# Row-halved output blocks in context attention, self-attention's last softmax steps reordered, and the gated weights' column sums in eight halves

## The chip, the cores and the metric

The kernel runs on one core of a Trainium2 chip. The metric is the device time of one execution in microseconds. The core's engines appear in the profile as PE (TensorE, matmuls; its weight loads are shown apart as PEld), DVE (VectorE), ACT (ScalarE), POOL (GpSimd) and SP (SyncE, whose queue issues nearly all DMAs here). Everything is in float32.

## The reference

The inputs are x (2 batches x 1024 tokens x 256) and a context of 2 x 154 rows of width 192. One transformer block is computed: self-attention with 16 heads of 64, attention over the context with 16 heads of 64, and a gated feed-forward part of inner width 1024, each behind a layer norm and with a residual.

```python
def _attention(xq, xkv, wq, wk, wv, wo, bo):
    q = (xq @ wq).reshape(B, S, N_HEADS, D_HEAD)
    k = (xkv @ wk).reshape(B, T, N_HEADS, D_HEAD)
    v = (xkv @ wv).reshape(B, T, N_HEADS, D_HEAD)
    attn = softmax(einsum('bihd,bjhd->bhij', q, k) * D_HEAD ** (-0.5), axis=-1)
    out = einsum('bhij,bjhd->bihd', attn, v).reshape(B, S, D_ATTN)
    return out @ wo + bo
h = _layernorm(x, ln1_g, ln1_b)
x = _attention(h, h, sa_wq, sa_wk, sa_wv, sa_wo, sa_bo) + x
h = _layernorm(x, ln2_g, ln2_b)
x = _attention(h, cond_emb, ca_wq, ca_wk, ca_wv, ca_wo, ca_bo) + x
h = _layernorm(x, ln3_g, ln3_b)
a, gate = split(h @ ff_w1 + ff_b1)
h = a * gelu(gate) @ ff_w2 + ff_b2
return h + x
```

## The kernel before

The order of every instruction on every engine is the order of the program text: the schedule is written out by hand, and nothing is moved by a planner. The stages are the first norm and projections, self-attention, context attention, and the feed-forward part. Stages overlap: steps of one are put between steps of its neighbours by lists of closures. `adds`, `stores`, `lates`, `side` and `later` are such lists. `stores` holds copies of finished PSUM banks to SBUF, `adds` the additions of finished output blocks to the residual, `later` DMAs that go out at most two a step, and `side` transposes of the next norm's output and other work of TensorE. `run_work(...)` runs what is due from these lists.

PSUM is divided into three pools. The pool of products has two banks (`mm_tile`): query projections, transposes. The pool of sums has two banks (`sum_tile`): output blocks, sums over steps. The pool of scores has two double banks. A tile of a pool waits until the tile two before it in that pool was read to the end.

**Self-attention** runs in 128 steps (SA = 128). The softmax of a step is spread over engines: `maxima` and `turn_group` (the transposes of the weighted exponentials, L733) on VectorE, `exponents` (L600) on ScalarE, `differences` and `softmax_join` (the denominators, L629) and `weighted` (L706) on GpSimd, `reciprocals` (L698) and `factors` on VectorE. The weighting of a step's second half may also run on ScalarE (`weighted_beside`). Its output projection (`out_rounds`, L547) is done in rounds of four blocks of 128 tokens. TensorE works there as an array of eight tiles of 64 rows x 32 columns: the two row halves (the two heads of a pair) write to two different banks at the same time. After a first crossing of each pair of banks, ScalarE reads one element of the first bank of the pair (`seen`, L556), and the second crossing then lets each row half add to the other's bank. So a round takes four banks, two of the sums and two of the products.

**Context attention** runs in units. A unit is a pair of heads of one batch: 16 units, batch 0 in units 0 to 7, batch 1 in units 8 to 15. A unit has three steps n = 0, 1, 2 that take 3, 3 and 2 blocks of 128 queries (CG). A step c = 3 ui + n issues its scores (`cross_first`, L999, K = 64 rows), the maxima over VectorE (L1004), the exponentials on ScalarE (L1017), and the weighting on GpSimd (L1028). The transposes follow two steps later (`cross_drain`), and the products with the values (`cross_values`, L1064, array of 32 x 64 tiles, four banks) come at step 0 two units later. Beside that, in the program's order:

- n = 0: the values of the unit two before, then a piece of `side`.
- n = 1: the query projection of the next unit (`cross_queries`, L411: 64 rows x 128 columns, two row halves at once on the two banks of the products), which ScalarE copies out (`take_both`, L426) at the next step.
- n = 2: an output piece, a value projection (even units), a piece of `side` or an output piece, the flush of the copies, and another output piece.

The output projection is cut into pieces of two blocks of 128 tokens (`out_piece`, L523: K = 128 rows, one bank of the sums, 8 matmuls for both blocks and both pairs of heads). Those of self-attention's last pairs of heads run in units 1 and 2, those of context attention's in later units, where an odd unit above 2 lists the pieces of the two units before (`cross_beside`), and those of the last two pairs in the feed-forward part. The bias and norm of the next stage can only start on a block once all its additions are made (`norm_beside`, the statistics on VectorE).

The context's values are projected with the 192 context columns as two halves of CC = 96 rows, `context_values(b, pr)` (L961), once per batch and even pair, eight times in all: one at self-attention's end and one in each even unit. ScalarE copies the result out (L968), and DMAs take it through memory in order to spread it over the four row groups that L1064 wants.

The **feed-forward** part computes 32 pairs of blocks with gates (L1169, 1187 to 1219) in 64 half steps k, and the second matrix by a Strassen-Winograd scheme (seven products for eight, final sums at L1289). For it VectorE forms four sums of quarters of ff_w2 (`column_sums`, L1256, 128 x 512 elements each) at k = 5 to 8. Statistics of the last norm of batch 1 run on VectorE in the half steps k = 10 and later.

## Time and profile before

| what | value |
|---|---|
| times of three runs | 1059.89, 1060.45, 1060.54 us (median 1060.45) |
| the profiled execution | 1060.44 us, its span 1058.6 us |
| busy share of the span | PE 99%, DVE 83%, POOL 73%, ACT 62% |
| context attention | first scores at 687.57 us of the span, last values at 900.44 us |

A line of the grouped view gives line, engine, operation, output <- inputs, tile (rows x columns in the array, where given), shape, count | busy us, mean ns of one | idle time before it and what ended it. A line of the timeline gives start and duration in us from the span's start, then engine, line, operation and the number of instructions that the row takes together; a bracket says how long the row's first instruction waited and for whom. Durations of matmuls of two row halves overlap, so their number times the mean is more than the time that they take together.

### The profile page before, as it was taken

The page shows a single profiled execution, that of the slowest core. Times are in us where ns is not written, and L with a number is a line of the kernel's source. Part 1 is how long each engine was busy: PE and PEld are TensorE (multiplying, and loading weights), DVE is VectorE, ACT ScalarE, POOL GpSimd, SP SyncE. Part 2 cuts the span into 40 slices and gives each one's busy share as a digit, 9 for nine tenths or more (in the row PEclk, how much of TensorE's full clock was granted, in tenths as well). Part 3 has the DMA queues.
Part 4 walks back from the last instruction along what each step waited for, and adds up shares of the span by engine and source line. Part 5 has one row for each costly group of instructions (what it writes and reads, how often), then busy time and mean ns, then how long its engine had stood idle before and what let it go on. Part 6 is the DMA issues. An engine that isn't in the chain of part 4 may idle for free.

```text
span 1058.6 us, 51303 instructions
## 1 busy us (share of the span) xinstructions
PE 1047.1 (99%) x21700; PEld 740.3 (70%) x21700; DVE 880.7 (83%) x1313; ACT 658.9 (62%) x2147; POOL 769.9 (73%) x1620
## 2 busy tenths in 40 slices
PE   8999999999999999999999999999999999999998
PEld 6456965556576666665786676666676667889997
DVE  5799999999899999999999999968776777675654
ACT  5776767777776766766776777666666655243221
POOL 2677777788778777777777777757665777598773
PEclk9999999999999999999999999999999999999999
DMA  4322221121121021122122012135323221000000
GB/s 106 95 65 60 50 61 42 45 54 34 25 54 45 15 54 45 29 44 55 24 44 50 21 39 56 49 104 132 101 59 83 69 59 41 1 11 11 21 11 30
DMA packets 96023, 52.87 MB, mean 50 GB/s; under 512 B 30314, under 2 KB 93810, under 8 KB 95794
## 3 DMA queue, kind: packets, MB, share of 16 engines
q1 hardware_dynamic: 94466, 48.93, 18.9%
q8 instruction: 171, 2.80, 1.1%
q10 hardware_dynamic: 1328, 0.66, 0.2%
q14 instruction: 58, 0.48, 0.1%
HBM read 36.23 MB, written 4.39 MB: 38 GB/s over the span
## 4 chain that ended last, share of the span: by engine, by line
PE 90%; DVE 4%; ACT 2%; POOL 2%; issue 1%; DMA 1%; SPq 0%; DVEq 0%; POOLq 0%; ACTq 0%
PE s L583 20%; PE po L639 20%; PE pv_sa L443 5%; PE py_ca L523 5%; PE pk_sa L411 5%; PE pq_sa L411 5%; PE pr L547 5%; PE pf L1289 5%; PE poc L1064 4%; PE pb L1169 4%; PE pq_ca L411 4%; PE sc L999 3%; PE pa L1169 2%; PE pc L1169 2%; PE ph_ln L323 1%
## 5 line engine op out<-in xcount | busy, mean ns | idle before, releaser
L600 ACT ACTIVATE p<-s,st 128x512 f32<-128x512 f32 x512 | 345.4, 685 | 152.8 <-DVE st L592 121.4
L706 POOL TENSOR_SCALAR p<-p,rd,ee 128x512 f32<-128x512 f32 x508 | 385.2, 768 | 75.5 <-DVE rd L698 75.1
L592 DVE TENSOR_REDUCE st<-s 128x2 f32<-128x1024 f32 x256 | 308.7, 1207 | 49.9 <-issue 16.1
L733 DVE STREAM_TRANSPOSE pT<-p 128x1024 f32<-128x1024 f32 x256 | 303.9, 1221 | 2.4 <-POOL p L706 2.3
L583 PE MATMUL s<-k_sa,q_sa 64*32 64x512 f32 x4096 | 256.7, 590 | 1.1 <-DVE k_sa L432 0.6
L639 PE MATMUL po<-pT,v_sa 64*32 64x256 f32 x6144 | 180.5, 376 | 1.7 <-ACT p L1017 1.6
L639 PEld LDWEIGHTS po<-pT,v_sa 64*32 64x32 f32 x6144 | 142.7, 106 | 45.0 <-issue 15.2
L583 PEld LDWEIGHTS s<-k_sa,q_sa 64*32 64x32 f32 x4096 | 102.8, 106 | 78.5 <-issue 51.4
L1017 ACT ACTIVATE p<-sc,neg 128x154 f32<-128x154 f32 x256 | 97.1, 406 | 72.2 <-DVE rden L1025 70.2
L1028 POOL TENSOR_SCALAR p<-p,rden 128x154 f32<-128x154 f32 x256 | 96.8, 399 | 52.9 <-DVE rden L1025 51.9
L600 ACT ACTIVATION_READ_ACCUMULATOR p<-s,st 128x1 f32 x512 | 103.0, 201 | 0.0
L1004 DVE TENSOR_REDUCE neg<-sc 128x6 f32<-128x924 f32 (+1 forms) x48 | 48.1, 1003 | 20.2 <-PE sc L999 20.0
L523 PE MATMUL py_ca<-ca_wo,o_ca 128*128 128x256 f32 x256 | 61.1, 385 | 0.0
L639 PE MATMUL po<-pT,third_v 64*32 64x256 f32 x2048 | 60.5, 376 | 0.0
L443 PE MATMUL pv_sa<-sa_wv,home 64*32 64x256 f32 x2048 | 60.2, 376 | 0.0
L443 PEld LDWEIGHTS pv_sa<-sa_wv,home 64*32 64x32 f32 x2048 | 48.4, 106 | 14.1 <-issue 5.4
L411 PE MATMUL pq_sa<-home,sa_wq 64*32 64x512 f32 (+1 forms) x976 | 58.0, 586 | 0.0
L411 PE MATMUL pq_ca<-home,ca_wq 64*128 64x512 f32 (+1 forms) x352 | 57.8, 589 | 0.0
L639 PEld LDWEIGHTS po<-pT,third_v 64*32 64x32 f32 x2048 | 46.6, 106 | 16.0 <-issue 4.6
L1017 ACT ACTIVATION_READ_ACCUMULATOR p<-sc,neg 128x1 f32 x256 | 56.5, 221 | 0.0
L627 POOL TENSOR_TENSOR zz<-ee,st 128x8 f32<-128x8 f32 x128 | 25.8, 202 | 42.1 <-ACT ee L625 42.1
L411 PE MATMUL pk_sa<-home,sa_wk 64*32 64x512 f32 x960 | 56.3, 589 | 0.0
(144 smaller groups left out, 1576.1 us busy)
## 6 DMA issues: line engine op xcount, KB each, us to landing
st<-st SPq DMA_DIRECT2D x510, 1.0 KB, 1.7
v_sa<-v_sa SPq DMA_DIRECT2D x24, 256.0 KB, 3.3
v_ca<-vd SPq DMA_DIRECT2D x32, 160.0 KB, 3.4
sa_wq<-in_L_xattn_sa_wq_dram SPq DMA_DIRECT2D x32, 128.0 KB, 3.3
sa_wk<-in_L_xattn_sa_wk_dram SPq DMA_DIRECT2D x32, 128.0 KB, 3.1
sa_wv<-in_L_xattn_sa_wv_dram SPq DMA_DIRECT2D x32, 128.0 KB, 3.3
ca_wq<-in_L_xattn_ca_wq_dram SPq DMA_DIRECT2D x32, 128.0 KB, 3.0
wf<-in_L_xattn_ff_w_dram SPq DMA_DIRECT2D x12, 256.0 KB, 4.8
```

The costliest lines, as they stand in the source:

```text
L411: nc.tensor.matmul(pq[r][f:f + m, at:at + n], lhsT=wt[own, c, f:f + m], rhs=h[own, c, t0:t0 + n], start=(c == 0), stop=(c == NH - 1), tile ...
L443: nc.tensor.matmul(pv[r][f:f + KB, i * VC:(i + 1) * VC], lhsT=h[own, c, t0:t0 + KB], rhs=wt[own, c, :], start=(c == 0), stop=(c == NH - 1) ...
L523: nc.tensor.matmul(py[:, e * D:(e + 1) * D], lhsT=o[:, i, (t + e) * P:(t + e + 1) * P], rhs=wo[kind, b, g][:, i, :], start=(i == 0), stop= ...
L583: nc.tensor.matmul(sc[a4 * KB:(a4 + 1) * KB, j, :], lhsT=q[r, c:c + KB], rhs=k[r, h * HB:(h + 1) * HB], start=True, stop=True, tile_positi ...
L592: nc.vector.tensor_reduce(st[:, 0, 0, i, :], sc, AX.X, ALU.max, negate=True)
L600: nc.scalar.activation(pr[:, j, :], sc[:, j, :], AF.Exp, bias=st[:, 0, 0, i, j:j + 1], accum_out=st[:, 0, 1, i, j:j + 1],)
L639: nc.tensor.matmul(po[a2][d:d + KB, :QH // 2], lhsT=v[r, t, e, d:d + KB], rhs=pT[r, d // DH * NK + n, :], start=(t == 0 and e == 0), stop= ...
L706: nc.gpsimd.tensor_scalar(pr[:, j, :], pr[:, j, :], v["rd"][:, c:c + 1], v["ee"][:, 0, c:c + 1], op0=ALU.mult, op1=ALU.mult,)
L733: nc.vector.transpose(halves[h][:, :, c:c + KB], slot[p]["members"][i].rearrange("p j (n k) -> p (j n) k", k=KB))
L1017: nc.scalar.activation(pr_[:, j, i, :T], sc[:, j, i * T:(i + 1) * T], AF.Exp, bias=neg[:, j, i:i + 1], accum_out=den[:, j, i:i + 1],)
L1028: nc.gpsimd.tensor_scalar(pr_[:, j, i, :T], pr_[:, j, i, :T], rden[:, j, i:i + 1], 1.0, op0=ALU.mult, op1=ALU.mult,)
L1169: nc.tensor.matmul(into[:, :BT], lhsT=lhs, rhs=wh[pair][i], start=first, stop=True, skip_group_check=True)
```

## The change

Five edits belong together.

1. `out_rounds` takes the kind of attention and a block width m. With m = P = 128 it does four blocks of tokens in 32 matmuls of 64 rows x 128 columns, two at a time, on the same four banks as in self-attention. `four_by_four` lists such rounds of four blocks. In units 1 and 2 (self-attention's last output; both rounds in unit 1, at n = 1 and n = 2), in units 7 to 11 (n = 2) and in unit 15 (n = 1) a round takes the place of the two pieces of two blocks. Where the next norm's transposes are due in that step (`beside`), in units 3 to 6 and 12 to 15, the step keeps pieces of 128 rows, and the side work runs at n = 2 only there. In the feed-forward part the pieces stay. The first crossings are issued behind the step's scores, the second crossings between the step's exponentials (`then(between)`: the first before the first head's exponentials and the second before the second head's), and the additions behind the step.
2. `context_values(pr, bank)` projects the values of both batches at once, with three pieces of 64 rows, the two row halves on two banks. That needs the context and its weights in another place: `context_beside` copies the context's columns to `both_ctx` by eight DMAs within SBUF, in units 3 to 6 of self-attention, and `load_weights` loads the value weights twice, for the two row halves. It is called four times, at self-attention's end and in units 2, 4 and 6. Batch 1's units only fetch their values from memory (`hold_values`, `spread_values`).
3. At self-attention's end the last two softmax steps (SA - 2 and SA - 1), which had been finished in context steps 0 and 1, are interleaved in another order: both reciprocals and weightings are issued in step 0, ahead of one or both transposes that had stood before them, and the last step's transposes move to the head of step 1, ahead of its maxima.
4. In unit 2's last step the output piece that had stood ahead of the value projection is gone with the first edit.
5. `column_sums` makes the four sums as eight halves of 128 x 256 elements, at k = 8 to 15.

```diff
@@ load_weights
-            wsl[kind, pr, what] = load_slice(f"{kind}_w{what}", pr * P, VC, CC)
+            t = wsl[kind, pr, what] = wpool.tile(
+                [P, DC // HR, VC], F32, tag="wv", name=f"{kind}_w{what}_{pr}")
+            own = w[f"{kind}_w{what}"][:, pr * P:pr * P + VC].rearrange("(c p) f -> p c f", p=HR)
+            for r0 in range(0, P, HR):
+                nc.sync.dma_start(out=t[r0:r0 + HR], in_=own)
@@
-    def out_rounds(b, g, tiles):
-        o = oT["sa", b, g]
+    def out_rounds(kind, b, g, tiles, m=KB):
+        o = oT[kind, b, g]
...
-                for f in range(0, P, KB):
+                for f in range(0, P, m):
                     for r in (1, 0):
                         at = 2 * pair + (r ^ swapped)
                         own, t0 = slice(r * HR, (r + 1) * HR), tiles[at] * P + f
                         nc.tensor.matmul(
-                            py[at][f:f + KB, :D], lhsT=o[own, i, t0:t0 + KB],
-                            rhs=wo["sa", b, g][own, i, :],
+                            py[at][f:f + m, :D], lhsT=o[own, i, t0:t0 + m],
+                            rhs=wo[kind, b, g][own, i, :],
...
+    rounds = []
+    def four_by_four(kind, b, g):
+        pairs = out_order(kind)
+        for i in range(0, len(pairs), 2):
+            rounds.append((kind, b, g, [t + e for t in pairs[i:i + 2] for e in range(2)]))
@@ turn_group
-        if i == 1:
+        slot[p]["left"] = slot[p].get("left", 2) - 1
+        if not slot[p]["left"]:
             del slot[p]
@@ self-attention's steps
+        if both and ui > SH - 2 and n in ((SH + 1, SH + 2) if ui % 2 else (0, 1)):
+            both.pop(0)()
@@
-    def context_values(b, pr, bank=mm_tile):
-        v = vs["ca", b, pr // 2] = pt_.tile([P, NB, VC], F32, tag="V", name=f"v_ca{b}_{pr}")
-        pv = bank(f"pv_ca{b}_{pr}")
-        for c in range(2):
-            nc.tensor.matmul(
-                pv[:, :VC], lhsT=ctxT[:, c, b * TP:b * TP + P],
-                rhs=wsl["ca", pr, "v"][:, c, :], start=(c == 0), stop=(c == 1),
-            )
+    both_ctx = ends[:, :DC // HR * P].rearrange("p (c k) -> p c k", k=P)
+    def context_beside():
...
+                    moves.append(lambda b=b, c=c, half=half, row=row, n=n, to=to: nc.sync.dma_start(
+                        out=both_ctx[to:to + n, c, :],
+                        in_=ctxT[row:row + n, half, b * TP:b * TP + P]))
...
+    def hold_values(b, pr):
+        v = vs["ca", b, pr // 2] = pt_.tile([P, NB + B, VC], F32, tag="V", name=f"v_ca{b}_{pr}")
+        return v
+    def spread_values(b, pr, at):
+        def back(a0):
+            for a4 in range(a0, a0 + 2):
+                nc.sync.dma_start(
+                    out=vs["ca", b, pr // 2][a4 * KB:(a4 + 1) * KB, :NB, :],
+                    in_=vd[b, pr].rearrange("(n p) d -> p n d", p=KB))
+        later.insert(at, lambda: back(0))
+        later.insert(at + 1, lambda: back(2))
+    def context_values(pr, bank):
+        v = hold_values(0, pr)
+        pv = [bank(f"pv_ca{b}_{pr}") for b in range(B)]
+        for c in range(DC // HR):
+            for b in range(B):
+                own = slice(b * HR, (b + 1) * HR)
+                nc.tensor.matmul(
+                    pv[b][:, :VC], lhsT=both_ctx[own, c, :], rhs=wsl["ca", pr, "v"][own, c, :],
+                    start=(c == 0), stop=(c == DC // HR - 1), tile_position=(b * HR, 0))
...
         def store():
+            for b in range(B):
+                nc.scalar.copy(v[:, NB + b, :], pv[b][:, :VC])
+            later.insert(0, lambda: [out(b) for b in range(B)])
+            spread_values(0, pr, 2)
@@ cross_first
-        def then(between=None):
+        def then(between=()):
...
-                if j and between:
-                    between()
+                for fn in between[j:j + 1] if len(between) > 1 else between if j else ():
+                    fn()
@@ cross_beside
-            out_pieces("ca", *divmod(ui // HP - 1, NQ), out_order("ca"))
+            four_by_four("ca", *divmod(ui // HP - 1, NQ))
@@ column_sums
-        t = half["t"]
+        n, part = divmod(n, 2)
+        t, own = half["t"], slice(part * NF // 4, (part + 1) * NF // 4)
...
+        nc.vector.tensor_tensor(into[:, own], x[:, own], y[:, own], ALU.subtract)
@@ the steps of context attention
-                out_pieces("sa", B - 1, NQ - 1, out_order("sa"))
+                four_by_four("sa", B - 1, NQ - 1)
...
-                load_weights("ca", nxt[1], "v")
+                if not nxt[0]:
+                    load_weights("ca", nxt[1], "v")
             flush(adds)
-            between = None
-            if c < 2:
-                if c == 0:
-                    turn_group(SA - 3, 1)
-                reciprocals(SA + c - 2)
-                factors(SA + c - 2)
+            between, taken = (), ()
+            if c == 0:
+                turn_group(SA - 3, 1)
+                reciprocals(SA - 2)
+                factors(SA - 2)
+            elif c == 1:
+                for i in range(2):
+                    turn_group(SA - 1, i)
             then = cross_first(c)
-            if c < 2:
-                weighted(SA + c - 2, 0)
-                weighted_beside(SA + c - 2, 1)
-                if c == 0:
-                    slot[SA - 1]["dd"] = differences(SA - 1, slot[SA - 1]["st"])
-                    between = lambda: softmax_join(SA - 1)
+            if c == 0:
+                weighted(SA - 2, 0, (0,))
+                weighted_beside(SA - 2, 1)
+                slot[SA - 1]["dd"] = differences(SA - 1, slot[SA - 1]["st"])
+                weighted(SA - 2, 0, (1,))
+                softmax_join(SA - 1)
             flush(stores)
             flush(lates)
             if n == 0 and ui > 1:
...
             else:
+                beside = n == 2 and side and side[0][0] and added.issuperset(side[0][1])
+                if rounds and (n == 2 or n == 1 and (ui == 1 or not nxt)):
+                    if beside:
+                        kind, ob, og, tiles = rounds.pop(0)
+                        out_pieces(kind, ob, og, tiles[::2])
+                    else:
+                        between, taken = out_rounds(*rounds.pop(0), P)
                 lates.append(then(between))
-            if c < 2:
-                turn_group(SA + c - 2, 0)
-                turn_group(SA + c - 2, 1)
+            if c == 0:
+                turn_group(SA - 2, 1)
+                reciprocals(SA - 1)
+                factors(SA - 1)
+                weighted(SA - 1, 0)
+                weighted_beside(SA - 1, 1)
+                turn_group(SA - 2, 0)
             cross_drain(c)
...
-                if ui == 1 or not nxt:
-                    run_work(2, 0)
-                else:
+                if ui > 1 and nxt:
                     run(lambda: cross_queries(*nxt))
                 run_work(0, 1)
             else:
                 run_work(0, 0, n_sum=1)
                 flush(adds)
-                if ui and ui % 2 == 0:
-                    run(lambda: context_values(*units[ui]))
-                run_work(0, 1, mm_tile)
+                if beside:
+                    run_work(0, 1, mm_tile)
                 flush(stores)
-                if ui > 1:
-                    run_work(0, 0, n_sum=1)
+                run_work(0, 0, n_sum=1)
+                if ui and ui % 2 == 0 and not b:
+                    run(lambda: context_values(ui, mm_tile))
+                elif b and ui % 2 == 0:
+                    hold_values(*units[ui])
+                    spread_values(*units[ui], 0)
...
+            adds.extend(taken)
@@ the feed-forward part's half steps
-            if len(CG) + 1 < k <= NF:
-                column_sums(k - len(CG) - 2)
+            if NF <= k < 2 * NF:
+                column_sums(k - NF)
```

More of the change, by code (lines that the diff above doesn't have):

```diff
@@ L807, in self_first @@
         return then
-    held, kept, rounds = [], [], []
+    held, kept = [], []
     def self_beside(ui):
@@ L828, in self_beside @@
             ob, og = divmod(ui // HP - 1, NQ)
-            for t0 in range(0, NG * 2, 2):
-                rounds.append(
-                    (ob, og, [t + e for t in out_order("sa")[t0:t0 + 2] for e in range(2)]))
+            four_by_four("sa", ob, og)
         if ui in (4, 6):
@@ L952, in context_ends @@
         return store
-    def context_values(b, pr, bank=mm_tile):
-        v = vs["ca", b, pr // 2] = pt_.tile([P, NB, VC], F32, tag="V", name=f"v_ca{b}_{pr}")
-        pv = bank(f"pv_ca{b}_{pr}")
-        for c in range(2):
-            nc.tensor.matmul(
-                pv[:, :VC], lhsT=ctxT[:, c, b * TP:b * TP + P],
-                rhs=wsl["ca", pr, "v"][:, c, :], start=(c == 0), stop=(c == 1),
-            )
-        def store():
-            own = one.tile([P, VC], F32, tag="own_v", name=f"own_v{b}_{pr}")
-            nc.scalar.copy(own, pv[:, :VC])
-            later.insert(0, lambda: nc.sync.dma_start(out=vd[b, pr][:P, :], in_=own))
-            def back(a0):
-                for a4 in range(a0, a0 + 2):
-                    nc.sync.dma_start(
-                        out=v[a4 * KB:(a4 + 1) * KB, :, :],
-                        in_=vd[b, pr].rearrange("(n p) d -> p n d", p=KB))
-            later.insert(2, lambda: back(0))
-            later.insert(3, lambda: back(2))
+    both_ctx = ends[:, :DC // HR * P].rearrange("p (c k) -> p c k", k=P)
@@ new lines, in context_beside @@
+    def context_beside():
+        moves = []
+        for b in range(B):
+            for c in range(DC // HR):
+                f = c * HR
+                while f < (c + 1) * HR:
+                    half, row = divmod(f, CC)
+                    n = min((c + 1) * HR - f, CC - row)
+                    to = b * HR + f - c * HR
+                    moves.append(lambda b=b, c=c, half=half, row=row, n=n, to=to: nc.sync.dma_start(
+                        out=both_ctx[to:to + n, c, :],
+                        in_=ctxT[row:row + n, half, b * TP:b * TP + P]))
+                    f += n
+        return moves
@@ L1419, in tile_transformer_block @@
                     hold_late_keys()
-                    run(lambda: context_values(*units[0]))
+                    run(lambda: context_values(0, mm_tile))
                     for pr in range(NKD, NPAIR):
```

18 lines of the change are left out of this document (13 added, 5 removed).

## The prediction

> **What bounds the kernel now.** I read the page's busy line first, then the groups of instructions by line and form, then the timeline of TensorE through context attention, with ScalarE and VectorE beside it where TensorE and they meet.
>
> ```profile
> PE 1047.1 (99%) x21700; PEld 740.3 (70%) x21700; DVE 880.7 (83%) x1313; ACT 658.9 (62%) x2147; POOL 769.9 (73%) x1620
> ```
> ```profile
> L523 PE MATMUL py_ca<-ca_wo,o_ca 128*128 128x256 f32 x256 | 61.1, 385 | 0.0
> ...
> L411 PE MATMUL pq_ca<-home,ca_wq 64*128 64x512 f32 x224 | 50.4, 589 | 0.0
> ...
> L556 ACT COPY seen<-pr 1x1 f32<-1x1 f32 x28 | 3.7, 132 | 0.0
> ```
>
> TensorE is busy for 1047.1 of 1058.6 us. The time is therefore its work plus every moment in which it waits, and any new wait of TensorE is paid in full. The profiled execution took 1060.44 us (span 1058.6, 1.84 outside it); the median of the three runs is 1060.45, so the sum below needs no correction.
>
> **The output rounds in units 7 to 11.** One unit of context attention, unit 7, in the timeline (start, duration, instruction), with two rows of unit 8:
>
> ```profile
> 778.51 2.41 PE L1064 MATMUL poc<-pT_ca,v_ca 32*64 32x256 f32 x80
> ...
> 785.18 0.69 PE L999 MATMUL sc<-k,q_ca 64*128 64x154 f32 x8
> ...
> 785.80 3.72 PE L523 MATMUL py_ca<-ca_wo,o_ca 128*128 128x256 f32 x16
> ...
> 786.16 1.11 ACT L426 ACTIVATE q_ca<-pq_ca 128x512 f32<-128x512 f32 x2
> ...
> 789.45 1.06 PE L999 MATMUL sc<-third_v,q_ca 64*128 64x154 f32 x12
> 790.44 2.41 PE L1064 MATMUL poc<-pT_ca,v_ca 32*64 32x256 f32 x80
> ...
> 799.55 1.03 PE L961 MATMUL pv_ca<-ca_wv,ctxT 96*128 96x256 f32 x4
> 800.42 1.89 PE L523 MATMUL py_ca<-ca_wo,o_ca 128*128 128x256 f32 x8
> ```
>
> The unit takes 790.44 - 778.51 = 11.93 us. A round replaces the 16 output instructions (3.65 us from 785.80 to 789.45) by 32 of half the rows, two at a time. Does that cost less? The 64-row queries take 50.4/224 = 0.225 us for 512 columns with two at once, so 0.225 us for a pair of 256 columns; the 128-row output takes 61.1/256 = 0.239 us. Sixteen pairs are 3.60 against 3.82 us: 0.22 us less, which I read as the price of changing between tile shapes, since the scores on either side are 64-row tiles already. I take 0.216 us for a pair, the step inside a block of one shape (four instructions from 799.55 to 800.42 take 0.87): 3.45 us for a round, and 0.20 saved. [...]
>
> Against it stands a bank. A round takes two banks of the pool of sums and two of the pool of products. The latter two hold the query projections, which ScalarE empties in the two copies at 786.16, until 787.27. The first quarter of a round, one crossing on the two free banks, starts at 785.18 + 0.59 = 785.77 and takes 3.45/4 = 0.86 us, until 786.63. The second quarter waits for 787.27 and some 0.06 us more. That is a wait of 0.7 us that the old form did not have, because its two blocks alternate on the pool of sums. That such waits are real is seen in unit 4, where the value projection asks for the first of those banks:
>
> ```profile
> 748.03 1.11 ACT L426 ACTIVATE q_ca<-pq_ca 128x512 f32<-128x512 f32 x2
> ...
> 748.71 1.13 PE L961 MATMUL pv_ca<-ca_wv,ctxT 96*128 96x256 f32 x4 [0.16 <-ACT q_ca L426]
> ```
>
> [...]
>
> Behind the waiting matmuls stand the rest of the round, the next scores and the next values; VectorE and ScalarE wait for those. The two "seen" copies (132 ns each) cost nothing here: the first follows the query copies, the second follows two exponentials and is due at about 788.4, before TensorE needs it at 789.0. Each round so costs 0.7 - 0.20 = +0.5. I take 0.47 for units 7 to 10: +1.9.
>
> Unit 11 is worse, because VectorE's norm statistics stand ahead of its maxima and the query copies come later:
>
> ```profile
> 827.94 2.41 PE L1064 MATMUL poc<-pT_ca,v_ca 32*64 32x256 f32 x80
> ...
> 834.61 0.69 PE L999 MATMUL sc<-third_v,q_ca 64*128 64x154 f32 x8
> ...
> 836.64 1.11 ACT L426 ACTIVATE q_ca<-pq_ca 128x512 f32<-128x512 f32 x2
> ...
> 839.86 3.02 PE L1064 MATMUL poc<-pT_ca,v_ca 32*64 32x256 f32 x80
> ```
>
> There the copies end 837.75 - 834.61 = 3.14 us after the scores start, and the second quarter wants to start after 1.45: 1.75 us of wait, less 0.2. In return the values after it took 3.02 instead of 2.41 because VectorE was late with statistics and sums; statistics no longer run at the unit's last step, so 0.6 comes back. Net +0.9; the statistics that move to unit 12 delay its query copies and make its transposes wait some 0.3. Together +1.2.
>
> **The value projections.** Eight projections of 96 rows twice become four of 64 rows three times, both batches side by side. One costs 0.87 us, as the pair of rows at 799.55 shows. The new one is six pairs, 6 x 0.216 = 1.30 us. Units 8, 10, 12 and 14 lose 0.87 each (-3.5); self-attention's end, units 4 and 6 gain 0.4 each (+1.2). Unit 2 is counted next. The eight added DMAs that copy the context, the doubled weight rows and the second batch's loads from memory are issued a unit (some 12 us) or more before their use, and on SyncE's queue they stand behind the exchange of their step: 0. If that cover is gone, an exchange comes late once or twice, a few tenths each; I see no gain in them.
>
> **Units 1 and 2.** All four blocks of self-attention's last output now lie in unit 1, and unit 2 keeps only its value projection, on the two banks that ScalarE has still to empty:
>
> ```profile
> 707.03 1.06 PE L999 MATMUL sc<-third_v,q_ca 64*128 64x154 f32 x12
> ...
> 715.30 2.41 PE L1064 MATMUL poc<-pT_ca,v_ca 32*64 32x256 f32 x80
> ...
> 721.97 0.69 PE L999 MATMUL sc<-third_v,q_ca 64*128 64x154 f32 x8
> ...
> 724.00 1.11 ACT L426 ACTIVATE q_ca<-pq_ca 128x512 f32<-128x512 f32 x2
> ...
> 726.41 0.45 ACT L968 COPY own_v<-pv_ca 128x256 f32<-128x256 f32 x1
> 726.72 2.59 PE L1064 MATMUL poc<-pT_ca,v_ca 32*64 32x256 f32 x80
> ```
>
> Before: 726.72 - 707.03 = 19.69. After, unit 1: scores 0.89, round 3.45, a wait of 0.2 for the second "seen" behind three exponentials, scores 0.59, round 3.45, scores 0.99: 9.57. Unit 2: scores end 7.26 after the values' start; the bank of the second batch comes free 725.11 - 715.30 = 9.81 after it; the three steps then left take 0.65, the scores 0.99: 11.5. Two value copies instead of one then hold the next values back by 0.5 where one held them by 0.18. In all 21.4: +1.7.
>
> **Unit 15** has its round at its second step, where three exponentials stand ahead of the second "seen":
>
> ```profile
> 883.07 3.72 PE L523 MATMUL py_ca<-ca_wo,o_ca 128*128 128x256 f32 x16
> ...
> 885.23 0.39 ACT L1017 ACTIVATE p<-sc,neg 128x154 f32<-128x154 f32 x1 [1.24 <-DVE rden L1025]
> ...
> 886.34 0.40 ACT L1017 ACTIVATE p<-sc,neg 128x154 f32<-128x154 f32 x1
> ...
> 886.73 0.79 PE L999 MATMUL sc<-k,q_ca 64*128 64x154 f32 x8
> ```
>
> The first three exponentials end at 886.34, "seen" at 886.5; the last quarter, due at 883.07 + 2.6 = 885.7, waits 0.9 and ends at 887.4, where 886.73 stood: +0.7, less 0.1 for the shape that no longer changes. +0.6.
>
> **Self-attention's end.** TensorE's longest wait is there:
>
> ```profile
> 692.20 2.37 DVE L733 STREAM_TRANSPOSE pT<-p 128x1024 f32<-128x1024 f32 x2 [0.34 <-POOL p L706]
> ...
> 693.78 0.20 POOL L629 TENSOR_TENSOR den<-zz 128x4 f32<-128x4 f32 x1
> ...
> 694.50 0.14 DVE L698 RECIPROCAL rd<-den 128x4 f32<-128x4 f32 x1
> ...
> 696.29 2.37 DVE L733 STREAM_TRANSPOSE pT<-p 128x1024 f32<-128x1024 f32 x2 [0.24 <-POOL p L706]
> ...
> 698.81 3.69 PE L639 MATMUL po<-pT,v_sa 64*32 64x256 f32 x128 [1.63 <-ACT p L1017]
> ```
>
> The last transposes end at 698.66 and TensorE starts at 698.81. In the new order the last denominators leave before the first exponentials (about 693.2, not 693.98), their reciprocals stand ahead of one of the two transposes at 692.20 instead of behind both (693.5, not 694.5), and the rest follows 1.0 us earlier. So -1.0; 0.6 of the wait stays. The maxima of the second scores now come behind the transposes, 2.7 us later; what hides that is the value block, which runs from 697.8 to 701.4. Without it: a few tenths.
>
> **Feed-forward.** VectorE's column sums:
>
> ```profile
> 917.56 0.59 PE L1169 MATMUL pa<-home,wf 128*128 128x256 f32 x2
> 918.29 0.70 PE L1169 MATMUL pb<-home,wf 128*128 128x256 f32 x2
> ...
> 918.49 0.84 DVE L1256 TENSOR_TENSOR w2s<-wf 128x512 f32<-128x512 f32 x1
> ...
> 922.25 0.48 DVE L1207 SCALAR_TENSOR_TENSOR own<-pb,cols,own 128x256 f32<-128x256 f32 x1 [0.44 <-PE pb L1169]
> ...
> 924.20 0.59 PE L1169 MATMUL pa<-home,wf 128*128 128x256 f32 x2
> 924.93 0.70 PE L1169 MATMUL pb<-home,wf 128*128 128x256 f32 x2
> ...
> 929.78 0.70 PE L1169 MATMUL pb<-hs,wf 128*128 128x256 f32 x2 [0.27 <-DVE own L1207]
> ```
>
> A product takes 0.43 (two instructions), so the next one at 918.29 came 0.3 us late: that is the whole sums' doing. Halves of about 0.4 fit into VectorE's idle 0.44 a step, so that goes. But the eight steps they now fill are those with the next norm's statistics, which already hold TensorE by 0.3 at 924.93 and as much or a little more at 929.78; with the slack gone each hold grows by 0.4. +0.8 - 0.4 = +0.4; bounds -0.4 and +2 (each half as long as the whole).
>
> **Sum.** +1.9 + 1.2 - 3.5 + 1.2 + 1.7 + 0.6 - 1.0 + 0.4 = +2.5; with the roundings kept, +2.4: 1062.8.
>
> **Rivals.** *The banks do not bind* (faster): if the query copies end within 1.45 us of the last scores, the five rounds lose their waits, 4 x 0.7 + 1.75 = 4.5: 1058.3. For it: unit 4 waited no more than 0.16 for the first bank; against it: unit 4 asked 2.8 us after its scores, and in unit 7 the copies end 2.09 after them, with nothing of the change ahead of them on ScalarE. 0.18. *The seen chain*: every swapped half waits for ScalarE, as forecast in units 1 and 15 only; 0.6 in six more rounds: 1066.4. Against it: two, not three, exponentials stand between. 0.1. *VectorE full in feed-forward*: halves nearly as long as wholes, +1.6 more: 1064.4. 0.11. *The reorder moves nothing*, since the delayed maxima hold the fourth scores instead: 1063.8. 0.09. Forecast: 0.52, its own range 1061.5 to 1064.
>
> **How the numbers follow.** The range reaches to the bank rival below and near the seen chain above: 1058.2 to 1065.8. A measurement of this kernel tells 0.2%, 2.1 us, from no change. The bank rival ends just beyond it, faster: 0.15 of its 0.18. The forecast lies 0.2 above the upper bound, 1062.6, so its chance falls on both sides: 0.23 within, 0.29 slower. The three other rivals are slower, 0.30. So 0.15 faster, 0.26 the same, 0.59 slower.
>
> **What would show it.** Right: TensorE idle before the second quarter of the rounds put down to the query copies (0.7 us in units 7 to 10, over 1.5 in unit 11), 2 us before unit 2's value projection, the wait at self-attention's end down to about 0.6. Wrong: rounds that run through in 3.5 us, a value projection in unit 2 that starts at once, or waits put down to "seen" in every round.

## The result, and the profile after

The changed kernel takes 1066.45 us (median of six runs, 1065.68 to 1068.24) where the kernel before took 1060.49 in the same comparison: ratio 1.0056, 95% interval 1.0043 to 1.0069. A second comparison, later, gave 1.0047 (1.0034 to 1.0060). It is slower by 5 to 6 us, where 2.4 were forecast, and it lies outside the range (1058.2 to 1065.8).

The profiled execution took 1065.68 us (span 1063.9), 5.24 us more than the profiled execution of the kernel before. It is the fastest of its six, so the places below add up to 0.7 us less than the medians differ. The page's busy line and groups of TensorE by line and form, after:

```profile
PE 1048.3 (99%) x21844; PEld 738.2 (69%) x21844; DVE 883.4 (83%) x1333; ACT 660.7 (62%) x2163; POOL 773.2 (73%) x1620
```
```profile
L527 PE MATMUL py_ca<-ca_wo,o_ca 128*128 128x256 f32 x160 | 38.5, 384 | 0.0
...
L551 PE MATMUL pr<-ca_wo,o_ca 64*128 64x256 f32 x192 | 25.9, 388 | 2.1 <-ACT q_ca L430 1.1 <-ACT seen L560 0.7
...
L1013 PE MATMUL pv_ca<-ca_wv,ends 64*128 64x256 f32 x48 | 7.4, 400 | 1.8 <-ACT q_ca L430 1.8
```

Of the 5.24 us, TensorE's busy time accounts for only 1.2. Its waits (waiting line, releaser: us in total, times, longest) have five entries of context attention and the feed-forward part that the kernel before did not have, or had in a smaller size:

```profile
PE pv_ca L1013 <- ACT q_ca L430: 1.8, 1, 1.8
...
PE pb L1215 <- DVE own L1253: 1.4, 2, 1.0
PE pr L551 <- ACT q_ca L430: 1.1, 1, 1.1
PE ph_ln L327 <- ACT q_ca L430: 1.0, 4, 0.3
PE pr L551 <- ACT seen L560: 0.7, 1, 0.7
```

Set side by side by the start of the same instructions, the two timelines give the change place by place. The forecast column is the prediction's own terms.

| stretch, from and to | before | after | change | forecast |
|---|---|---|---|---|
| start to unit 1's first scores | 702.43 | 701.25 | -1.18 | -0.6 |
| to unit 3's second scores | 26.82 | 30.10 | +3.28 | +1.7 |
| unit 3, to unit 4's second scores | 12.36 | 12.83 | +0.47 | 0 |
| unit 4, to unit 5's second scores | 13.65 | 14.58 | +0.93 | +0.4 |
| units 5 and 6, to unit 7's second scores | 25.60 | 26.02 | +0.42 | +0.4 |
| units 7 to 10 (four rounds, two projections gone) | 49.42 | 49.38 | -0.04 | +0.15 |
| unit 11, to unit 13's first scores | 22.44 | 22.86 | +0.42 | +0.3 |
| units 13 and 14, to unit 15's second scores | 29.37 | 28.50 | -0.87 | -0.9 |
| unit 15, to the first gated product | 11.79 | 12.46 | +0.67 | +0.6 |
| gated products, to the first final sum | 40.42 | 41.57 | +1.15 | +0.4 |

Three places carry the miss: units 1 and 2 (+1.6), units 3 and 4 (+1.0), the feed-forward part (+0.75). The timeline of TensorE at the first of them:

```profile
722.14 0.69 PE L1045 MATMUL sc<-third_v,q_ca 64*128 64x154 f32 x8
724.64 1.84 PE L1013 MATMUL pv_ca<-ca_wv,ends 64*128 64x256 f32 x11 [1.81 <-ACT q_ca L430]
...
726.38 2.06 PE L1045 MATMUL sc<-third_v,q_ca 64*128 64x154 f32 x10
728.37 3.05 PE L1110 MATMUL poc<-pT_ca,v_ca 32*64 32x256 f32 x80
731.35 1.06 PE L1045 MATMUL sc<-third_v,q_ca 64*128 64x154 f32 x12
```

The wait of 1.81 us before the value projection was forecast. What follows was not: ten score instructions take 2.06 us where twelve took 1.06 before, and the values 3.05 where 2.59. No wait stands at either. The table by stretch shows why (columns: stretch, its length, busy time and instructions of each engine, then the granted TensorE clock, DMA share, GB/s):

```profile
720.00:726.00 6.00, 4.19 (x30) 2.53 (x28) 5.38 (x15) 4.24 (x20) 3.95 (x10) 1.00 0.00 0
726.00:727.00 1.00, 1.00 (x13) 0.98 (x11) 0.00 (x0) 0.88 (x6) 0.94 (x3) 0.67 0.00 0
727.00:728.00 1.00, 1.00 (x9) 1.00 (x6) 0.00 (x0) 0.31 (x1) 1.00 (x4) 0.50 0.31 102
728.00:729.00 1.00, 1.00 (x18) 0.53 (x25) 0.52 (x1) 0.00 (x0) 1.00 (x3) 0.50 0.65 199
729.00:730.00 1.00, 1.00 (x40) 0.63 (x32) 0.69 (x2) 0.28 (x1) 0.32 (x2) 0.63 0.69 116
730.00:735.00 5.00, 5.00 (x82) 3.05 (x68) 3.48 (x10) 2.71 (x14) 2.72 (x8) 1.00 0.98 228
```

The granted clock falls to one half at about 726.3 and is back at about 729.7; at half the clock 3.4 us hold 1.7 us of work. The fall begins 1.7 us after the wait's end, and a wait that was priced at its length costs about twice that here.

In the feed-forward part two idle times of TensorE have grown. Before, they were 0.14 us (924.20 + 0.59 to 924.93, in the prediction's rows) and 0.27. After:

```profile
929.20 0.70 PE L1215 MATMUL pb<-home,wf 128*128 128x256 f32 x2 [0.58 <-DVE own L1237]
...
935.03 0.70 PE L1215 MATMUL pb<-hs,wf 128*128 128x256 f32 x2 [1.04 <-DVE own L1253]
```

Behind them stand the half sums on VectorE. Their group after, and the group of the whole ones before:

```profile
L1309 DVE TENSOR_TENSOR w2s<-wf,w2s 128x256 f32<-128x256 f32 x4 | 3.0, 756 | 0.0
L1309 DVE TENSOR_TENSOR w2s<-wf 128x256 f32<-128x256 f32 x4 | 2.4, 596 | 0.0
```
```profile
L1256 DVE TENSOR_TENSOR w2s<-wf,w2s 128x512 f32<-128x512 f32 x2 | 1.8, 912 | 0.0
L1256 DVE TENSOR_TENSOR w2s<-wf 128x512 f32<-128x512 f32 x2 | 1.5, 762 | 0.0
```

Eight halves take 5.4 us, four wholes took 3.3. The forecast had a half at 0.4. Single halves do take 0.41, others 0.91; VectorE and GpSimd of the same moments tell them apart:

```profile
924.56 0.42 DVE L1237 TENSOR_TENSOR own<-pb,own 128x256 f32<-128x256 f32 x1
...
925.27 0.91 DVE L1309 TENSOR_TENSOR w2s<-wf,w2s 128x256 f32<-128x256 f32 x1
...
930.73 0.91 DVE L1309 TENSOR_TENSOR w2s<-wf,w2s 128x256 f32<-128x256 f32 x1
...
935.23 0.41 DVE L1309 TENSOR_TENSOR w2s<-wf 128x256 f32<-128x256 f32 x1
```
```profile
924.48 0.73 POOL L1200 TENSOR_TENSOR home<-home 128x256 f32<-128x256 f32 x1
925.17 0.73 POOL L1201 TENSOR_TENSOR hs<-home,hs 128x256 f32<-128x256 f32 x1
...
930.63 0.73 POOL L1258 TENSOR_TENSOR third_v<-own 128x256 f32<-128x256 f32 x1
```

Each slow half starts while a GpSimd instruction of 128x256 elements runs, and ends 0.28 us after it (925.27 + 0.91 = 926.18 against 925.17 + 0.73 = 925.90; 931.64 against 931.36); that holds for six of the eight, and the two of 0.41 start when none of that size runs. An addition of the same size whose one operand lies in a PSUM bank (`own<-pb,own`, 0.42) is not held by the GpSimd instruction that runs at its side. Of the whole sums before, two took 0.68 and 0.69 us, and the two of 1.13 and 0.84 ended 0.55 us after such an instruction. As the rows stand, a sum of two SBUF operands waits for it, whole or half, and eight small ones meet more of them (six) than the four large ones did (two). This is read from the rows; no run took GpSimd's part away.

### The profile page after: what moved, and what is told of

It reads as the page before. It is cut to its first block, busy times and chain, and to the rows that moved or that the text cites. A ratio compares the mean times of both kernels' runs of the same rounds, so it can differ in the third digit from the quotient of the medians.

```text
span 1063.9 us, 51640 instructions
## 1 busy us (share of the span) xinstructions
PE 1048.3 (99%) x21844; PEld 738.2 (69%) x21844; DVE 883.4 (83%) x1333; ACT 660.7 (62%) x2163; POOL 773.2 (73%) x1620
## 4 chain that ended last, share of the span: by engine, by line
PE 84%; DVE 6%; ACT 3%; POOL 2%; issue 2%; DMA 1%; SPq 1%; DVEq 0%; POOLq 0%; ACTq 0%
PE po L651 20%; PE s L595 19%; PE pr L551 7%; PE pv_sa L447 5%; PE pk_sa L415 5%; PE pf L1337 4%; PE pq_sa L415 4%; PE poc L1110 4%; PE pb L1215 3%; PE py_ca L527 3%; PE pa L1215 2%; PE pc L1215 2%; PE sc L1045 2%; ACT p L1063 2%; PE pq_ca L415 2%
## 5 line engine op out<-in xcount | busy, mean ns | idle before, releaser
L595 PE MATMUL s<-k_sa,q_sa 64*32 64x512 f32 x4096 | 255.6, 590 | 1.1 <-DVE k_sa L436 0.6
L595 PEld LDWEIGHTS s<-k_sa,q_sa 64*32 64x32 f32 x4096 | 100.9, 106 | 79.6 <-issue 49.8
L551 PE MATMUL pr<-sa_wo,o_sa 64*32 64x256 f32 (+1 forms) x1856 | 59.8, 377 | 0.0
L415 PE MATMUL pq_sa<-home,sa_wq 64*32 64x512 f32 (+1 forms) x976 | 57.9, 586 | 0.0
L415 PE MATMUL pq_ca<-home,ca_wq 64*128 64x512 f32 (+1 forms) x352 | 57.8, 589 | 0.0
L551 PEld LDWEIGHTS pr<-sa_wo,o_sa 64*32 64x32 f32 (+1 forms) x1856 | 47.2, 109 | 14.4 <-issue 5.1
L651 PEld LDWEIGHTS po<-pT,third_v 64*32 64x32 f32 x2048 | 44.3, 106 | 17.8 <-issue 5.4
L415 PE MATMUL pk_sa<-home,sa_wk 64*32 64x512 f32 x960 | 56.0, 589 | 0.0
```

Of the source, the lines that this page charges most:

```text
L415: nc.tensor.matmul(pq[r][f:f + m, at:at + n], lhsT=wt[own, c, f:f + m], rhs=h[own, c, t0:t0 + n], start=(c == 0), stop=(c == NH - 1), tile ...
L551: nc.tensor.matmul(py[at][f:f + m, :D], lhsT=o[own, i, t0:t0 + m], rhs=wo[kind, b, g][own, i, :], start=swapped == 0 and i == 0, stop=swap ...
L595: nc.tensor.matmul(sc[a4 * KB:(a4 + 1) * KB, j, :], lhsT=q[r, c:c + KB], rhs=k[r, h * HB:(h + 1) * HB], start=True, stop=True, tile_positi ...
L651: nc.tensor.matmul(po[a2][d:d + KB, :QH // 2], lhsT=v[r, t, e, d:d + KB], rhs=pT[r, d // DH * NK + n, :], start=(t == 0 and e == 0), stop= ...
```

## The experiments

Executions of one kernel spread by some 0.4% (the kernel before: 1059.65 to 1064.14 us in one comparison). Most of that arises in self-attention, of which the change touches only eight added DMAs and the end: context attention's first scores start between 687.45 and 691.21 us in these profiles. Behind that point the same instructions stand at the same distances to 0.1 us in every profile, where no edit and no fall of the clock lies between, so where a median hides a difference the place is told beside it.

**The wait in unit 2 covered.** Three products that nothing reads, ahead of the projection:

```diff
+                if ui == 2:
+                    fill = sum_tile("fill")
+                    for i in range(3):
+                        nc.tensor.matmul(fill[:, :D], lhsT=..., rhs=..., start=True, stop=True)
                 if ui and ui % 2 == 0 and not b:
                     run(lambda: context_values(ui, mm_tile))
```

> The changed kernel, with three extra 128-row products (six instructions, about 1.4 us) on a free bank of the sums, issued in unit 2 just ahead of its value projection; nothing reads their result. They fall into the 1.8 us in which TensorE waits for the query copies, and take nothing off any chain. Theory A (the wait lets the clock fall): the granted clock stays at full speed after unit 2, unit 3's scores and values take about 0.9 + 2.4 us instead of 2.3 + 3.0, and the kernel is about 1.7 us faster than the changed one, some 1064.7. Rival (the clock falls for another reason): the fall stays and the time is the changed kernel's, 1066.4, or 0.1 to 0.3 more.

```profile
726.48 1.56 PE L1564 MATMUL fill<-sa_wo,o_sa 128*128 128x256 f32 x6
728.36 1.83 PE L1013 MATMUL pv_ca<-ca_wv,ends 64*128 64x256 f32 x11 [0.31 <-ACT q_ca L430]
...
730.08 1.11 PE L1045 MATMUL sc<-third_v,q_ca 64*128 64x154 f32 x10
731.12 2.41 PE L1110 MATMUL poc<-pT_ca,v_ca 32*64 32x256 f32 x80
```

The scores are back at 1.11 us and the values at 2.41; this place is 1.61 us shorter, with no work taken away and some added. But one profile does not show that the cover did it. In the profile of whole sums (below) the wait stands uncovered, the clock does not fall, and the place is just as short (28.49 us in both):

```profile
725.15 1.83 PE L1013 MATMUL pv_ca<-ca_wv,ends 64*128 64x256 f32 x11 [1.80 <-ACT q_ca L430]
...
726.87 1.11 PE L1045 MATMUL sc<-third_v,q_ca 64*128 64x154 f32 x10
727.91 2.41 PE L1110 MATMUL poc<-pT_ca,v_ca 32*64 32x256 f32 x80
```

So the 1.61 us are the price of the fall, and the wait brings it only in some executions; that it takes the wait is told by counting them (below). With the cover, the mean granted clock was 1.0 in all six. The median, 1067.21, ratio 1.0047 (1.0035 to 1.0059), did not come down to the 1064.7 expected: only the executions in which the clock fell can gain, about 1.0 us on the mean, and that is within the two intervals.

**The piece back in unit 2.** The second half of self-attention's last output as two pieces, one in unit 1, one ahead of the value projection:

```diff
-                    if beside:
+                    if beside or ui == 1 and n == 2:
...
-                run_work(0, 0, n_sum=1)
+                if ui > 1:
+                    run_work(0, 0, n_sum=1)
```

> The changed kernel, with the second half of self-attention's last output (two of the four blocks in unit 1's last step, two in unit 2) as two pieces of 128 rows again, placed as before: one in unit 1's last step, one in unit 2's ahead of the value projection. Theory A (the missing piece costs unit 2 its cover, and the wait costs the clock): the wait of 1.8 us and the fall of the clock both go, 1.8 + 1.7 us, so about 3.3 us faster than the changed kernel, 1063.1. Rival (only the wait goes, the clock falls anyway): 1.6 us faster, 1064.8.

```profile
722.67 1.99 PE L527 MATMUL py_sa<-sa_wo,o_sa 128*128 128x256 f32 x8
724.72 1.83 PE L1013 MATMUL pv_ca<-ca_wv,ends 64*128 64x256 f32 x11
...
726.44 1.11 PE L1045 MATMUL sc<-third_v,q_ca 64*128 64x154 f32 x10
727.48 2.41 PE L1110 MATMUL poc<-pT_ca,v_ca 32*64 32x256 f32 x80
```

No wait, no fall of the clock; 1065.69 us, ratio 1.0032 (1.0021 to 1.0042). By place it is 3.0 us shorter than the changed kernel up to unit 3's second scores: 1.3 for the wait and 1.6 for the clock. This is theory A's number, up to 0.3, against an execution in which the clock fell.

**Whole column sums at half steps 5 to 8**, as before:

```diff
-        n, part = divmod(n, 2)
...
-            if NF <= k < 2 * NF:
-                column_sums(k - NF)
+            if len(CG) + 1 < k <= NF:
+                column_sums(k - len(CG) - 2)
```

> The changed kernel with the column sums as four whole ones again at half steps 5 to 8. Theory B (the halves cost the feed-forward part 1.15 us, by their stalls and by standing in the steps with the norm's statistics): from the first product of the feed-forward part to the first final sum 40.4 us again instead of 41.6, 1.15 us faster than the changed kernel, 1065.3. Rival (the statistics held TensorE there anyway): less than 0.3 us faster.

From the first gated product (896.79) to the first final sum (937.14) are 40.35 us, 1.22 less than the changed kernel's 41.57: theory B, and not the rival. The median, 1066.68 (ratio 1.0041, 1.0025 to 1.0058), hides it in the executions' spread.

**Halves, but at half steps 5 to 8**, two a step:

```diff
+            if len(CG) + 1 < k <= NF:
+                for part in range(2):
+                    column_sums(2 * (k - len(CG) - 2) + part)
```

> The changed kernel with its eight half column sums at half steps 5 to 8 again, two a step, where the four whole ones stood. Theory B1 (a half costs as much as 0.6 to 0.7 us because it meets a GpSimd instruction, wherever it stands): the eight take over 4.5 us of VectorE where the four whole ones took 3.3, and the stretch from the first product of the feed-forward part to the first final sum is 41.0 us or more. Rival B2 (only the place is wrong, beside the statistics): the halves take about 0.4 us each, 3.3 in all, and the stretch is 40.4 us as before.

```profile
L1309 DVE TENSOR_TENSOR w2s<-wf,w2s 128x256 f32<-128x256 f32 x4 | 2.2, 598 | 0.0
L1309 DVE TENSOR_TENSOR w2s<-wf 128x256 f32<-128x256 f32 x4 | 2.2, 586 | 0.0
```

Neither expectation holds. The halves take 0.59 us each, 4.4 in all, and the stretch (899.55 to 940.36) is 40.81 us. Of the 1.2 us that the edit costs, 0.4 to 0.5 come from the halves being halves and 0.8 from their place beside the statistics, where they also meet more of GpSimd. That split rests on one execution.

**Pieces of 128 rows in units 7 to 11 and 15**, no rounds there:

```diff
-                    if beside:
+                    if beside or rounds[0][0] == "ca":
...
+                elif not nxt:
+                    run_work(2, 0)
```

> The changed kernel with pieces of 128 rows in place of the five rounds in units 7 to 11 and of the one in unit 15; the round pair in unit 1 stays. Theory C (a round's second quarter waits for the query copies, a crossing in unit 15 for the exponentials): units 7 to 10 come out 0.4 us shorter each, units 11 and 12 together 0.9, unit 15 0.7, so 3.2 us faster than the changed kernel, 1063.2. Rival (the rounds are cheap, and what these units lost is lost to the statistics that moved): less than 1 us faster, and units 7 to 10 within 0.1 us of what they are.

Place by place it is theory C: units 7 to 10 come out 0.42 us shorter each, unit 11 1.5 and unit 15 0.66; 3.8 us together, a little more than the 3.2 expected. 1063.87 us, ratio 1.0013 (1.0003 to 1.0024). The waits that the rounds had are best seen on the weight loads, since a matmul row spans them (unit 7 of the changed kernel):

```profile
789.50 0.76 PEld L551 LDWEIGHTS pr<-ca_wo,o_ca 64*128 64x128 f32 x8
790.75 0.29 PEld L551 LDWEIGHTS pr<-ca_wo,o_ca 64*128 64x128 f32 x2 [0.50 <-ACT q_ca L430]
791.24 2.45 PEld L551 LDWEIGHTS pr<-ca_wo,o_ca 64*128 64x128 f32 x22 [0.19 <-ACT seen L560]
```

Eight loads, the first quarter; then 0.50 us for the query copies and 0.19 for "seen".

**The converse: a wait put into the kernel before.** Unit 2's value projection ahead of its piece:

```diff
-                run_work(0, 0, n_sum=1)
+                if ui != 2:
+                    run_work(0, 0, n_sum=1)
                 flush(adds)
                 if ui and ui % 2 == 0:
                     run(lambda: context_values(*units[ui]))
+                if ui == 2:
+                    run_work(0, 0, n_sum=1)
```

> The kernel before, with the value projection of unit 2 moved ahead of that step's output piece: the same work, but the projection now waits for the query copies. Theory A (a wait of some 1.8 us lets the clock fall in about half of the executions): a wait of about 1.9 us, and in about half the runs a mean granted clock of 0.998 and 1.6 us more; so 1.9 or 3.5 us slower than before. Rival (the clock falls because of the half-row work of units 1 and 2 in the changed kernel, which this kernel does not have): 1.9 us slower and a clock of 1.0 in every run.

```profile
726.17 1.69 PE L961 MATMUL pv_ca<-ca_wv,ctxT 96*128 96x256 f32 x4 [2.01 <-ACT q_ca L426]
727.66 3.06 PE L523 MATMUL py_sa<-sa_wo,o_sa 128*128 128x256 f32 x8
730.65 1.06 PE L999 MATMUL sc<-third_v,q_ca 64*128 64x154 f32 x12
```
```profile
728.00:729.00 1.00, 1.00 (x4) 0.73 (x3) 0.00 (x0) 0.35 (x2) 1.00 (x3) 0.50 0.00 0
```

The same work in another order waits 2.01 us, and the projection then takes 1.69 instead of 1.13, the piece 3.06 instead of 1.99, at half the clock. By place it is 3.2 us up to unit 3's second scores; in the median it is 1064.03 us, ratio 1.0021 (1.0012 to 1.0030). In 4 of 10 executions the mean granted clock was 0.998; their mean is 1064.8, that of the others 1063.7. The rival falls: none of the row-halved output rounds stands here.

**The changed kernel again.**

> The changed kernel once more, beside the kernel that follows. [...]

Three of five executions had a clock of 0.998. With those of the first comparison, 7 of 11: their mean is 1067.05, that of the other four 1066.02, a difference of 1.0 us, smaller than the 1.6 of the place but of its sign. The other kernels with both kinds have 2.4 (whole sums), 1.5 (pieces) and 1.1 us (values first); weighted by their numbers of executions, the four give 1.4. Over all kernels that have the wait of 1.8 to 2.0 us (the changed one, whole sums, early halves, pieces, values first), the clock fell in 21 of 40 executions; over all that do not have it (64 executions of the kernel before beside these, and 49 of the kernels that cover the wait) the mean was 0.998 in none. In eleven of these 113 it was 0.999. A fall at the very end may be what gives that, by the author's estimate: in the profile of the kernel with the statistics in every last step (below) the clock falls 1.0 us before the end of the span, behind TensorE's last product.

The profiles also show where the fall comes. In the four that have one in unit 2 (the changed kernel twice, early halves, values first) it begins 1.69, 1.66, 0.92 and 0.43 us after the wait's end, and another fall begins behind the last product, 337.92 us after the first in all four: 99 times 3.413 us, the length of the fall in the clock record of the changed kernel's trace. So the two falls of each of these executions lie on a grid of 3.413 us. With the grid counted on from them, an estimate, the stretch ahead of the fall in unit 2 held 1.72, 1.76, 1.80 and 2.01 us of the wait. Counted back from the fall at the end, the grid cuts the wait of 1.8 us in whole sums into 1.53 and 0.27, and in pieces into 0.41 and 1.40; there the clock stayed up. An estimate from these numbers, if the wait meets any place of the grid alike: a wait of 1.81 us puts at least 1.72 us into one stretch in 52% of executions, and at least 1.63, the wait that never brought a fall, in 58%. Of the 30 executions with the wait of 1.8 us, 17 had the fall.

**What is left of the change put together**: the reordered steps, the projection for both batches, whole sums, pieces, and the piece ahead of unit 2's projection.

> What the readings leave as gains: the reordered softmax steps, the value projection for both batches at once, whole column sums at half steps 5 to 8, pieces of 128 rows everywhere in context attention but for the one round in unit 1's second step, and a piece ahead of unit 2's value projection. By the places of the two traces: -1.2 at self-attention's end, +0.3 in units 1 and 2, +0.5 in unit 3 for statistics that now run in its second step, +0.9 and +0.4 in units 4 and 6, -3.5 in units 8 to 14 for the four projections gone: 2.6 us faster than before (ratio 0.9975). Rival (the projections gone are replaced by waits for VectorE, as in unit 11): no faster than before.

1059.74 us against 1061.80 for the kernel before beside it: ratio 0.9984 (0.9974 to 0.9994), faster by 1.7 us where 2.6 were expected. By place, from context attention's first scores to the first final sum, it is 2.6 shorter.

**The same with the statistics in every last step:**

```diff
-                if beside:
+                if not taken:
                     run_work(0, 1, mm_tile)
```

> The same as the combined kernel, but the norm's statistics may run in every unit's last step again where no round is taken (as before). If the 0.5 us of unit 3 and the 0.2 us waits of the transposes for the query copies come from the statistics' move: another 0.5 us faster, some 3.1 us faster than before (ratio 0.997). Rival (those waits come from the later value projection): the same time as the combined kernel.

1059.87 us, ratio 0.9982 (0.9973 to 0.9991). Unit 3's 0.44 us is gone, as expected, and at unit 15 it stands 2.89 us ahead of the kernel before, in a span of 1055.7; unit 4's 0.9 stays. The medians of the two combined kernels cannot be told apart.

**The projection ahead of the transposes** (the same, with the call of `context_values` moved before `run_work(0, 1, mm_tile)`):

> The combined kernel with the statistics in every last step, and with the value projection of units 2, 4 and 6 ahead of the next norm's transposes, where the kernel before has it, not behind the last piece. By the rows: in unit 4 the 0.33 us of the shape's change and the 0.19 us wait for the transposes' bank go, and a wait of 0.2 us for the query copies comes, so units 4 and 6 together 0.3 to 0.5 us shorter than in the combined kernels and about 3.3 us faster than before (ratio 0.997). Rival (the projection merely takes over the transposes' wait): the same place to place.

```profile
749.68 2.05 PE L1013 MATMUL pv_ca<-ca_wv,ends 64*128 64x256 f32 x12 [0.16 <-ACT q_ca L430]
752.01 0.63 PE L327 MATMUL ph_ln<-ident,xn_ln 128*128 128x128 f32 x4 [0.28 <-ACT v_ca L1022]
```

Worse: the transposes now wait for the copies of the values, of which there are two, on both banks. Units 4 and 6 get 0.5 and 0.9 longer, and the ratio is 0.9997 (0.9989 to 1.0006). Both expectations fail.

## Why the prediction was wrong, and where it was right

- **Units 1 and 2.** The working was right up to the wait: 1.81 us before the projection, put down to the query copies, and 1.67 of the 3.28 us measured are the 1.7 forecast. The step that failed is the price of that wait. It was taken at its length; in the profiled execution it also halved the clock for 3.4 us and cost 1.6 more. The prediction's sum has no term for the clock; the longest wait that it shows, 1.63 us in the kernel before, had no such consequence. Filled, reordered and inserted waits, by the count of executions, show the cause from three sides.
- **Feed-forward.** The term was mis-sized: +1.15 for +0.4. A half was taken at 0.4 us, and took 0.68 on the mean, because it waits for GpSimd as the rows read. That is most of the way to the rival "VectorE full in feed-forward" (+2.0), and for its stated reason, halves nearly as long as wholes. The runs split the cost into 0.4 to 0.5 for the halves and 0.8 for their place, where the prediction had +0.8 for the place and -0.4 for smaller pieces.
- **Units 3 and 4.** Forecast at 0 and +0.4, measured +0.47 and +0.93. The prediction saw that the statistics leave the last step for unit 12 but not that they do so in unit 3 too, where they delay the query copies and let the transposes wait 0.28; the combined kernel with the statistics back loses that. In unit 4 the projection comes last, behind a change of shape and a wait for VectorE's copies of the transposes (0.33 and 0.19 us on its first weight loads; the profile names no releaser for the first), and takes 1.76 us instead of the 1.30 forecast. This is read from the rows, and no run bears it out: the one that moved the projection made unit 4 longer.
- **Rounds.** Right: 0.42 a unit against 0.47, with the wait at the second quarter. The terms were less good than their sum: the query copies held unit 7's round 0.50 us, not 0.7, and "seen", put at nothing there, another 0.19; the work itself so saved about 0.27 (0.69 less 0.42) for the 0.20 forecast. Unit 11's wait (1.53 on the weight loads, 1.13 on the matmuls) was shorter than the 1.75 worked out, and its cost to unit 13's first scores +0.42 against +0.3. Unit 15 +0.67 against +0.6, put down to "seen". The rival that the banks do not bind falls, and so does that of the seen chain, with 0.19 for its 0.6 a round.
- **Projections gone** (-0.87 each) and **the reorder** (TensorE's wait at self-attention's end from 1.63 to 0.57 us) right within 0.2. That the whole first stretch gained 1.18 for 0.6 is chance: the projection there cost its share (1.50 us for 0.97, some 0.1 more behind it), but self-attention ran 0.75 us shorter ahead of it.

```profile
696.37 0.69 PE L1045 MATMUL sc<-third_v,q_ca 64*128 64x154 f32 x8
697.63 1.74 PE L651 MATMUL po<-pT,v_sa 64*32 64x256 f32 x55 [0.57 <-DVE pT L745]
```

The sum of the places explains the span of the profiled execution to 0.1 us. The change's good parts are the reorder and the four projections gone, 4.7 us by place; the rounds, the halves, the uncovered projection and what follows from them cost 9.9.

## What to carry to other kernels

Price a wait of a busy TensorE by what stands after it as well, and cover a wait of about 2 us with useful work: the 1.81 us in unit 2 cost 1.6 us more behind them, and with a cover the mean granted clock was 1.0 in all six executions. Row-halved tiles saved little here (about 0.27 us a round), where the neighbours already have that shape, and the two banks more that they take are free only when someone has emptied them (0.50 us of wait for the query copies in unit 7). Splitting a two-operand VectorE instruction in two did not halve its cost beside a busy GpSimd (0.68 us on the mean for a half, 0.84 for a whole); look at where the pieces end against GpSimd's rows.

## What the runs showed of the hardware

A wait of 1.8 to 2.0 us in an otherwise busy stream came with a mean granted clock of 0.998 in 21 of 40 executions, and that mean never came in 113 without it; in the four profiles that show the fall, the clock is at one half for 3.41 us. The wait of 1.63 us in the kernel before did not do so. What besides the wait's length decides it is not shown. On the grid of 3.413 us, a stretch with 1.72 us of the wait in unit 2 was followed by a fall and one with 1.53 was not, but at the end of the kernel before and of "the piece back in unit 2", behind products of 128 rows, 1.73 and 1.89 us on the same grid brought no fall yet. Nor do the profiles of the kernel before and the changed one show a fall for the 1.9 us ahead of TensorE's very first instruction.

Two executions of the changed kernel differ by 1.9 us at context attention's first scores (687.45 and 689.33), and all profiles by up to 3.8, with the same waits of TensorE ahead of them at both ends of that range (the changed kernel and pieces). In the slower of these two, TensorE's rows of two lines appear interleaved (L415 and L595 in turn from 402.26 to 402.45 us), as if the row halves ran apart. What sets them apart is open.
